# The first two pairs of a graph kernel in one written order on all engines

## The chip, the cores and the metric

The kernel runs on one core of one Trainium2 chip. The metric is the device time of one execution in microseconds; less is better. The engines of the core work side by side, each through its own list of instructions: TensorE (PE; its weight loads are shown apart as PEld), VectorE (DVE), ScalarE (ACT), GpSimd (POOL) and SyncE (SP, which here only issues transfers). An instruction that needs the result of another engine waits on a semaphore at the head of its own list.

## The reference, cut to what matters

The input is x with 128 graphs of 64 nodes and 768 features, and an integer adjacency of 128 x 64 x 64. There are two layers. The change lies in the first:

```python
h = relu(layernorm(x))
ctx  = (A @ (h @ Wadj.T + badj)) / deg + (A.T @ (h @ Wrev.T + brev)) / rdeg + h @ Wself.T + bself
rel  = (sum over j of A * E[rels]) @ Wr.T  + br * deg      # relation ids are the adjacency values
rel += (the same for the transposed adjacency) @ Wrr.T + brr * rdeg
x = x + ctx + rel
```

The second layer (attention over the graph and a gate) follows in a second phase that the change leaves alone.

## The kernel before

Rows are taken in tiles of 128 (two graphs), and tiles in pairs; there are 32 pairs. In the first phase each pair needs:

- `prep` and `prep_c`: the adjacency as float and bf16, and what the counting of relation ids needs;
- `norm` and `relu`: statistics of the tile on VectorE, a power on GpSimd, the relu on ScalarE;
- `degrees`: one small product on TensorE that sums the adjacency; then a reciprocal, and `over_degrees` writes the divided adjacency into `r`;
- `operands(p, k, q)`: TensorE multiplies h by r (so that the aggregation comes before the weights), ScalarE copies the result from PSUM; six such sets for a pair give the blocks a00 to a12 of the left operand A;
- `count`, `digits`, `count_t`: how often each relation id occurs in each row, on VectorE, then transposed by TensorE, so that the relation term becomes a product of counts with a small table;
- the products of A (2 x 3 blocks) with the weights B (3 x 3 blocks, three weight matrices side by side). From the second pair on this takes 15 block products instead of 18, with sums of blocks: `form` makes sums of A's blocks, `sum_of_weights` sums of B's blocks, once, in place. The first pair uses 18 plain products, since the sums aren't there yet.

```python
# (A block, B block, PSUM bank, first?, C block to add when done, sign, with counts?)
PRODUCTS = (("f1", "g6", "a", True, "11", "+", False), ("f7", "g10", "b", True, "00", "-", False), ...)
PLAIN = tuple((f"a{k}{j}", f"b{j}{q}", "abcdab"[2 * q + k], j == 0, f"{k}{q}" if j == 2 else None,
               "+", False) for q in range(3) for j in range(3) for k in range(2))
```

PSUM is divided: four banks a to d for the products, and two buffers `pb` that operands, degrees, count transposes and the table share. `add` takes a finished bank into x on VectorE:

```python
nc.tensor.matmul(bank[b][:, :CQ], OPS[p, an][:, q, s, :], bw[bn][...], ...)   # line 613
...
nc.vector.tensor_add(v, bank[b][:, :CQ], v)                                  # line 605 (607: minus)
```

`merged(main, side)` writes the six steps of each product down in order, and slips each side item in before the step whose number it names. A scheduler may then reorder the instructions of an engine; within `manual_schedule(engines=...)` those engines keep the written order. Before, only VectorE's first few instructions were held so:

```python
load(0)                       # adjacency and both x tiles of pair 0
nc.scalar.dma_start(et, e_t); # and five bias rows, on ScalarE's queue
for n in ("b00", "b10", "b20", "b01"): load_block(n)
load(1)
for n in ("b11", "b21", "b02", "b12", "b22"): load_block(n)
nc.sync.dma_start(wrt[0], wr_t); nc.sync.dma_start(wrt[1], wrr_t)
...
with tc.manual_schedule(engines={mybir.EngineType.DVE}):
    prep(0); deviation(X[0], ...); rd = degrees(0); scaled_mean(...)
    over_degrees(0, rd); deviation(X[1], ...); scaled_mean(...)
for k in range(2): relu(k, to[k])
operands(0, 0, 0); operands(0, 1, 0); prep_c(0)
late = ([(8 + 6 * i, operands(0, k, q)) for the other four sets]
        + [(20, build_table), (22, count(0, 0)), (24, count(0, 1)), (26, digits(0)),
           (60, count_t(0, 0)), (60, count_t(0, 1))]
        + [(i, sum_of_weights(bw, n)) for i, n in ((21, "g10"), (38, "u"), (45, "g12"), ...)])
for p in range(NP):
    more = [(3, finish(p - 1, ...))] if p else late
    merged(main(p), own(p) + side(p + 1) + more)
```

(Lambdas are written here as plain calls.) `build_table` scales the embedding rows (es), multiplies them by two weight tables and adds the biases: six float products into a `pb` buffer, a copy by ScalarE, then three bf16 parts split off by VectorE (a cast and a subtraction for each) and sent by SyncE into `tab`.

Of the kernel before, what the change touches and what calls it, by code (L numbers as in the profile page):

```python
# [72 lines left out]
PLAIN = tuple((f"a{k}{j}", f"b{j}{q}", "abcdab"[2 * q + k], j == 0, f"{k}{q}" if j == 2 else None,  # L73
               "+", False) for q in range(3) for j in range(3) for k in range(2))
# [58 lines left out]
def kernel(  # L133
# [104 lines left out]

    ident = const.tile([P, P], F32, name="ident")
# [115 lines left out]
    with ExitStack() as px:  # L355
# [7 lines left out]
        def load(p):  # L363
            if p >= NP:
                return
            AI[p] = work.tile([P, 2, 2, N], I32, name="ai")
            for d, src in ((0, adj), (1, adj_t)):
                nc.sync.dma_start(
                    AI[p][:, :, d, :],
                    src[p * 2 * GT : (p + 1) * 2 * GT].rearrange("(t g) i j -> (g i) t j", g=GT))  # L370
            for t in (2 * p, 2 * p + 1):
                X[t] = keep.tile([P, D], F32, name="x", bufs=6)
                nc.sync.dma_start(X[t], xf[t * P : (t + 1) * P, :])

        wrt = [keep.tile([P, D], F32, name="wrt", tag="x", bufs=6) for i in range(2)]
        load(0)
        et = wa.tile([P, NREL], F32, name="et")
        nc.scalar.dma_start(et, e_t)

        bia = keep.tile([5, D], F32, name="bia", tag="hf", bufs=2)  # L380
        for i, v in enumerate((br, brr, badj, brev, bself)):
            nc.scalar.dma_start(bia[i : i + 1, :], row(v, 1))

# [8 lines left out]
        for n in ("b00", "b10", "b20", "b01"):  # L392
            load_block(n)
        load(1)
        for n in ("b11", "b21", "b02", "b12", "b22"):
            load_block(n)
        nc.sync.dma_start(wrt[0], wr_t)
        nc.sync.dma_start(wrt[1], wrr_t)
        identb = wa.tile([P, P], BF16, name="identb")
        nc.vector.tensor_copy(identb, ident)  # L400
# [3 lines left out]
        for g in range(GT):  # L404
            s = slice(g * N, (g + 1) * N)
            nc.vector.memset(blkb[s, s], 1.0)

        vals = wa.tile([P, NG, N], BF16, name="vals")
        nc.gpsimd.iota(vals, pattern=[[1, NG], [0, N]], base=1, channel_multiplier=0,
                       allow_small_or_imprecise_dtypes=True)  # L410
        rts = []
        for i in range(2):
            r = wa.tile([P, 2, 3, N], F32, name=f"r{i}")
            for k in range(2):
                nc.vector.tensor_copy(r[:, k, 2, :], idc)
            rts.append(r)

# [3 lines left out]
        def build_table():  # L421
            ids = wa.tile([P, NV], F32, name="ids")
            nc.gpsimd.iota(ids, pattern=[[1, NV]], base=1, channel_multiplier=0,
                           allow_small_or_imprecise_dtypes=True)
            es = wa.tile([P, 2, NROW], F32, name="es")
            nc.gpsimd.memset(es, 0.0)
            for d in range(2):
                nc.vector.tensor_mul(es[:, d, d * NV : (d + 1) * NV],
                                     et[:, d * NB + 1 : (d + 1) * NB], ids)


            eb = wa.tile([5, NROW], F32, name="eb")
            nc.gpsimd.memset(eb, 0.0)
            nc.gpsimd.iota(eb[0:1, 0:NV], pattern=[[1, NV]], base=1, channel_multiplier=0,
                           allow_small_or_imprecise_dtypes=True)
            ebr = wa.tile([1, NROW], F32, name="ebr")
            nc.gpsimd.memset(ebr, 0.0)
            nc.gpsimd.iota(ebr[0:1, NV:NCNT], pattern=[[1, NV]], base=1, channel_multiplier=0,
                           allow_small_or_imprecise_dtypes=True)
            nc.sync.dma_start(eb[1:2, :], ebr)  # L440
            nc.sync.dma_start(eb[2:5, NCNT:NROW], ident[0:3, 0:3])
            pt = pss.tile([P, 2, 512], F32, name="pb")
            for hf in range(2):
                s = slice(hf * HALF, (hf + 1) * HALF)
                for d in range(2):
                    nc.tensor.matmul(pt[:NROW, hf, :HALF], es[:, d, :], wrt[d][:, s],
                                     start=(d == 0), stop=False)
                nc.tensor.matmul(pt[:NROW, hf, :HALF], eb, bia[:, s], start=False, stop=True)
            v = keep.tile([P, D], F32, name="tv", tag="hf", bufs=2)
            qs = work.tile([P, 2, D], BF16, name="tq", tag="eq", bufs=1)  # L450
            ql = keep.tile([P, D], BF16, name="tl", tag="hf", bufs=2)
            nc.scalar.copy(v[:NROW].rearrange("p (a b) -> p a b", a=2), pt[:NROW, :, :HALF])
            for i in range(3):
                q = qs[:, i] if i < 2 else ql
                nc.vector.tensor_copy(q[:NROW], v[:NROW])
                if i < 2:
                    nc.vector.tensor_sub(v[:NROW], v[:NROW], q[:NROW])
                for (a, b), tab in zip(PARTS, tabs):
                    nc.sync.dma_start(tab[i : 3 * (b - a) : 3, :], q[a:b, :])
# [8 lines left out]
        def norm(t):  # L468
            to = small.tile([P, 2], F32, name="rn")
            stats(X[t], to, behind=(t // 2 == 2))  # L470
            relu(t, to)

        def prep(p):

            af = ADF[p] = work.tile([P, 2, 2, N], F32, name="af", bufs=1)
            ins = nc.vector.tensor_copy(af, AI[p])
            if p == 2:
                tc.keep_in_program_order(ins)
            ab = AB[p] = work.tile([P, 2, 2, N], BF16, name="ab", bufs=1)
            nc.vector.tensor_copy(ab, af)  # L480
# [31 lines left out]

        def over_degrees(p, rd):

            nc.vector.reciprocal(rd, rd)
            for d in range(2):
                nc.vector.tensor_mul(rts[p % 2][:, :, 1 - d, :], ADF[p][:, :, d, :], rd[:, :, d, :])  # L517

        def count(p, k):

            eq = work.tile([P, 2, NG, N], BF16, name="eq", bufs=1)
            ins = nc.vector.tensor_tensor(
                eq, GR[p][:, k, :, None, :].to_broadcast([P, 2, NG, N]),
                vals[:, None, :, :].to_broadcast([P, 2, NG, N]), op=OP.is_equal)
            if p < 2 and k == 0:
                tc.keep_in_program_order(ins)
            nc.vector.tensor_tensor(
                eq, eq, WO[p][:, k, :, None, :].to_broadcast([P, 2, NG, N]), op=OP.mult)
            nc.vector.tensor_reduce(SUM[p][:, k], eq, AX.X, OP.add)
# [54 lines left out]
        def main(p):  # L584
# [44 lines left out]
            rest_of = ["12"] if p else ["12", "01", "11", "10", "00", "02"]  # L629
# [23 lines left out]

        def side(p):

            if p >= NP:
# [5 lines left out]
                    (9, lambda: over_degrees(p, degrees(p))),  # L662
# [15 lines left out]
        def own(p):  # L678

            if p == 0:  # L680
                return []
            return [(0, lambda: form(p, "f5", "f6", "f3")),
                    (10, lambda: form(p, "f10")),
                    (18, lambda: form(p, "f11"))]
# [3 lines left out]
        with tc.manual_schedule(engines={mybir.EngineType.DVE}):  # L688
            prep(0)
            to = [small.tile([P, 2], F32, name="rn") for k in range(2)]  # L690
            mv = [small.tile([P, 2], F32, name="mv") for k in range(2)]
            deviation(X[0], to[0], mv[0])
            rd = degrees(0)
            scaled_mean(to[0], mv[0])
            over_degrees(0, rd)
            deviation(X[1], to[1], mv[1])
            scaled_mean(to[1], mv[1])
        for k in range(2):
            relu(k, to[k])
        operands(0, 0, 0)  # L700
        operands(0, 1, 0)
        prep_c(0)
        late = ([(8 + 6 * i, lambda k=k, q=q: operands(0, k, q)) for i, (k, q) in enumerate(
                    ((0, 1), (1, 1), (0, 2), (1, 2)))]
                + [(20, build_table), (22, lambda: count(0, 0)),
                   (24, lambda: count(0, 1)), (26, lambda: digits(0)),
                   (60, lambda: count_t(0, 0)), (60, lambda: count_t(0, 1))]
                + [(i, lambda n=n: sum_of_weights(bw, n)) for i, n in (
                    (21, "g10"), (38, "u"), (45, "g12"), (50, "g6"), (54, "g14"), (60, "v"), (75, "w"),
                    (85, "g3"), (88, "g9"), (91, "g5"), (94, "g8"), (97, "g1"), (100, "g11"))])  # L710
        for p in range(NP):
            more = [(3, lambda: [f() for k in range(2) for f in finish(p - 1, k)])] if p else late
            if p == 1:
                more.append((10, row_constants))
            if p == NP - 1:
                more += fetch()
            merged(main(p), own(p) + side(p + 1) + more)


    with ExitStack() as px:  # L720
# [203 lines left out]
        def one_over(t):  # L924
            nc.vector.reciprocal(DN[t], DN[t])
# [161 lines left out]
        def parsed(order):  # L1087
            return [(n, int(k or 0)) for n, _, k in (x.partition("/") for x in order)]

        px.enter_context(tc.manual_schedule(engines={  # L1090
            mybir.EngineType.PE, mybir.EngineType.DVE, mybir.EngineType.Activation,
            mybir.EngineType.Pool}))
# [62 lines left out]
```

## Time and profile before

| | |
|---|---|
| time, median of 3 runs | 2501.05 us (2500.21 to 2501.13) |
| span of the profiled execution | 2500.9 us |
| TensorE busy | 2465.1 us, 99% |
| VectorE busy | 1972.9 us, 79% |
| ScalarE busy | 1073.7 us, 43% |
| first main product of pair 0 begins | 18.41 us |
| first main product of pair 2 begins | 137.33 us |
| VectorE busy from 0 to 137.33 us | 119.42 us |

A line of the order of time gives the start, the length, the engine, the line of the kernel, the operation, what it writes and reads, the shapes and how many instructions are put together; in brackets stands how long the engine was idle before it and which instruction released it. A float product of 256 columns is two records on TensorE. A line of a stretch gives its bounds and length, then busy us and instructions of PE, PEld, DVE, ACT and POOL, the mean granted clock of TensorE, the busy share of the transfer engines and GB/s.

### The profile page before, as it was taken

How to read it: one execution, taken by the hardware profiler on the slowest of the kernel's cores; microseconds unless marked ns; L12 is line 12 of the kernel's file. 1: busy time of each engine (PE TensorE's matmuls, PEld its weight loads, DVE VectorE, ACT ScalarE, POOL GpSimd, SP SyncE). 2: the span in 40 equal slices, each digit the busy share in tenths (PEclk: the TensorE clock that was granted, in tenths of full speed). 3: DMA queues.
4: the chain of work that ended last, by engine and by line, in shares of the span. 5: the costliest groups of instructions: out<-in, count | busy, mean ns of one | idle time of the engine just before them, and what ended most of it. 6: DMA issues, size and time to landing. Idle time of an engine off the chain costs nothing. (4 is left out here: it accounts for less than half of the span.)

```text
span 2500.9 us, 35441 instructions
## 1 busy us (share of the span) xinstructions
PE 2465.1 (99%) x12108; PEld 1730.6 (69%) x12108; DVE 1972.9 (79%) x4112; ACT 1073.7 (43%) x3588; POOL 439.5 (18%) x799
## 2 busy tenths in 40 slices
PE   7999999999999999999999999999999999999997
PEld 5888888888888888888888885444444444444445
DVE  7978677677777777776777655888888888888888
ACT  2122222222222222222222214777777777777777
POOL 0122121121121211211211201111111111111122
PEclk9999999999999999999999999999999999999998
DMA  5112122121131121221211243344444444444434
GB/s 181 55 65 94 53 84 75 53 103 56 53 106 53 59 100 53 78 81 53 93 66 51 102 132 128 97 110 109 109 104 110 104 104 104 113 108 104 106 88 95
DMA packets 116215, 224.58 MB, mean 90 GB/s; under 512 B 36554, under 2 KB 49981, under 8 KB 116034
## 3 DMA queue, kind: packets, MB, share of 16 engines
q1 hardware_dynamic: 106152, 197.48, 24.3%
q0 software_dynamic: 9728, 24.78, 6.4%
q8 instruction: 95, 1.56, 0.3%
q14 instruction: 86, 0.70, 0.1%
q10 hardware_dynamic: 154, 0.06, 0.0%
HBM read 96.07 MB, written 100.66 MB: 79 GB/s over the span
## 5 line engine op out<-in xcount | busy, mean ns | idle before, releaser
L613 PE MATMUL pwa<-weights,op 128*128 128x256 f32 x2304 | 542.1, 382 | 1.1 <-DVE x L605 1.1
L613 PEld LDWEIGHTS pwa<-weights,op 128*128 128x128 f32 x2304 | 423.3, 190 | 69.6 <-DVE x L605 9.0
L574 ACT COPY op<-pb 128x768 f32<-128x768 f32 x160 | 124.3, 798 | 753.9 <-PE pb L566 753.9
L613 PE MATMUL pwb<-weights,op 128*128 128x256 f32 x1536 | 369.4, 381 | 0.0
L308 DVE TENSOR_TENSOR op<-op 128x768 f32<-128x768 f32 x248 | 231.2, 952 | 153.5 <-ACT op L574 153.3
L613 PEld LDWEIGHTS pwb<-weights,op 128*128 128x128 f32 x1536 | 284.3, 190 | 45.8 <-issue 7.0
L806 PE MATMUL pma<-weights,op_f 128*128 128x512 f32 x620 | 307.6, 593 | 0.3 <-DVE weights L833 0.3
L858 ACT ACTIVATE pr<-pr 128x128 f32<-128x128 f32 x768 | 225.4, 296 | 25.0 <-DVE pr L848 24.9
L806 PE MATMUL pmb<-weights,op_f 128*128 128x512 f32 x372 | 191.2, 595 | 0.0
L806 PEld LDWEIGHTS pma<-weights,op_f 128*128 128x128 f32 x620 | 111.8, 190 | 112.9 <-issue 104.3
L282 POOL TENSOR_TENSOR rn<-ve,mhalf 128x1 f32<-128x1 f32 x128 | 107.6, 841 | 458.2 <-DVE ve L281 458.1
L613 PE MATMUL pwc<-weights,op 128*128 128x256 f32 x780 | 187.1, 383 | 0.0
L613 PE MATMUL pwd<-weights,op 128*128 128x256 f32 x768 | 178.5, 381 | 0.0
L566 PE MATMUL pb<-r,h 64*128 64x192 f32 x1536 | 155.4, 340 | 10.4 <-DVE r L517 7.2
L613 PEld LDWEIGHTS pwc<-weights,op 128*128 128x128 f32 x780 | 145.7, 190 | 25.3 <-issue 6.7
L545 POOL COPY c<-cnt 128x243 bf16<-128x243 bf16 x64 | 44.9, 731 | 663.0 <-PE pb L553 611.4
L613 PEld LDWEIGHTS pwd<-weights,op 128*128 128x128 f32 x768 | 146.2, 191 | 20.4 <-issue 0.7
L276 DVE BATCH_NORM_STATS2 st<-x 128x6 f32<-128x384 f32 x256 | 134.5, 547 | 30.7 <-DMA x<-in_x_dram 29.2
L566 PEld LDWEIGHTS pb<-r,h 64*128 64x128 f32 x1536 | 125.1, 189 | 47.0 <-issue 42.5
L643 ACT ACTIVATE hf<-x,rn 128x768 f32<-128x768 f32 x64 | 65.8, 1027 | 188.8 <-issue 128.3
L858 ACT ACTIVATION_READ_ACCUMULATOR pr<-pr 128x1 f32 x768 | 144.3, 188 | 0.0
L645 POOL TENSOR_TENSOR x<-x,hf 128x768 f32<-128x768 f32 x64 | 116.3, 1817 | 95.3 <-ACT hf L643 95.3
(207 smaller groups left out, 4280.3 us busy)
## 6 DMA issues: line engine op xcount, KB each, us to landing
x<-in_x_dram SPq DMA_DIRECT2D x64, 384.0 KB
h<-hf SPq DMA_DIRECT2D x64, 384.0 KB
out_dram<-x SPq DMA_DIRECT2D x64, 384.0 KB
hh<-hh SPq DMA_DIRECT2D x64, 384.0 KB
h<-h SPq DMA_DIRECT2D x64, 384.0 KB
x<-hh SPq DMA_DIRECT2D x64, 384.0 KB
out_dram<-f POOLq DMA_DIRECT2D x62, 384.0 KB, 5.2
hx<-weights SPq DMA_DIRECT2D x88, 192.0 KB
```

Of the source, the lines that this page charges most:

```text
L276: ins = nc.vector.bn_stats(st[:, i, :], src[:, i * HALF : (i + 1) * HALF])
L282: nc.gpsimd.tensor_tensor(to[:, 0:1], ve, mhalf, op=OP.pow)
L308: return (nc.vector.tensor_add if s1 == "+" else nc.vector.tensor_sub)(to, x, y)
L545: nc.gpsimd.tensor_copy(c3, CNT[p][:, k, :, None].to_broadcast([P, NROW, 3]))
L566: nc.tensor.matmul(ps[:, g, i * 3 * N : (i + 1) * 3 * N], H0[t][s, kb * P : (kb + 1) * P], rts[p % 2][s, k].rearrange("p s n -> p (s n)"), ...
L574: nc.scalar.copy(a.rearrange("p h s (g n) -> p g (h s) n", g=GT), ps[:, :, : 6 * N].rearrange("p g (x n) -> p g x n", n=N))
L613: nc.tensor.matmul(bank[b][:, :CQ], OPS[p, an][:, q, s, :], bw[bn][:, (s * KQ + q) * CQ : (s * KQ + q + 1) * CQ], start=(first and q == s ...
L643: nc.scalar.activation(h, X[t], AF.Relu, scale=to[:, 0:1], bias=to[:, 1:2])
L645: nc.gpsimd.tensor_add(X[t], X[t], h)
L806: nc.tensor.matmul(bank[p, b], OPS[p, an][:, q, :], bw2[bn][:, 2 * q * CQ : 2 * (q + 1) * CQ], start=(first and q == 0), stop=(q == KQ - 1 ...
L858: nc.scalar.activation(PR[t][:, j, h, :], PR[t][:, j, h, :], AF.Copy, accum_out=to)
```

## The change

Four things are done at once, all in the first two pairs:

1. The whole beginning, up to the end of the second pair's products, is written in one order for TensorE, VectorE, ScalarE, GpSimd and the issues of SyncE; from the third pair on the scheduler orders as before. Each side item has a place of its own in one of two lists (`first`, `second`).
2. The table products come before the first main product, between the first operand sets; the casts of the three parts go from VectorE to ScalarE. The loads they need (table weights, biases) go ahead of the weights, all on SyncE.
3. The 18 plain products run C block by C block (three in a row finish a block in one bank), columns in the order 0, 2, 1. Four of the six C blocks take their counts at once; two at the end of the pair, where all six did before.
4. The counting is cut in two (`ids_worth`, `ids_sum`), and reciprocal and scaled mean are placed apart.

It is meant to begin the main products with less in front of them, and to leave no hole between them while counts, sums and operands are made.

```diff
-               "+", False) for q in range(3) for j in range(3) for k in range(2))
+PLAIN = tuple((f"a{k}{j}", f"b{j}{q}", "abcdab"[2 * i + k], j == 0, f"{k}{q}" if j == 2 else None,
+               "+", i > 0) for i, q in enumerate((0, 2, 1)) for k in range(2) for j in range(3))
...
+    in_order = {PE, DVE, Activation, Pool}
+    written.enter_context(tc.manual_schedule(engines=in_order | {mybir.EngineType.SP}))
...
+        nc.scalar.dma_start(et, e_t)
+        load_adj(0)
+        load_x(0)
         nc.sync.dma_start(wrt[0], wr_t)
         nc.sync.dma_start(wrt[1], wrr_t)
+        for i, v in enumerate((br, brr, badj, brev, bself)):
+            nc.sync.dma_start(bia[i : i + 1, :], row(v, 1))
...
+        nc.sync.dma_start(eb[2:5, NCNT:NROW], ident[0:3, 0:3])
+        nc.sync.dma_start(eb[1:2, :], ebr)
+        load_block("b00")
+        load_x(1)
+        for n in ("b10", "b20", "b02", "b12"):
+            load_block(n)
+        load(1)
+        for n in ("b22", "b01", "b11", "b21"):
+            load_block(n)
...
-                nc.vector.tensor_copy(q[:NROW], v[:NROW])
+            nc.scalar.copy(q[:NROW], v[:NROW])
...
-            rest_of = ["12"] if p else ["12", "01", "11", "10", "00", "02"]
+            rest_of = ["12"] if p else ["00", "10"]
...
+        prep(0); scaled_rows(); rd = degrees(0); to, mv = deviations((0,)); one_over(rd)
+        mean_and_relu(0, to[0], mv[0]); over_degrees(0, rd)
+        table_product(0); operands(0, 0, 0); table_product(1); table_product(2); table_copy()
+        operands(0, 0, 1); prep_c(0); to, mv = deviations((1,))
...
+        first = [(0, ids_worth(0, 0)), (1, mean_and_relu(1, ...)), (2, ids_sum(0, 0)),
+            (4, operands(0, 0, 2)), (8, count(0, 1)), (12, operands(0, 1, 0)), (12, operands(0, 1, 1)),
+            (17, operands(0, 1, 2)), (18, table_part(0)), (19, weights_sums("g10")),
+            (20, table_part(1)), (22, digits(0)), (23, prep(1)), (24, devs(1)), (26, table_part(2)),
+            (28, degrees_and_norms(1)), (30, weights_sums("w", "v")), (36, weights_sums("g6")),
+            (38, weights_sums("u", "g14")), (38, count_t(0, 0)), (40, prep_c(1)), (44, count(1, 0)),
+            (45, count_t(0, 1)), (52, count(1, 1)), (54, operands(1, 1, 2)), ...]
+        second = [(0, form(1, "f5", "f6", "f3")), (7, prep(2)), (7, weights_sums("g9")),
+            (10, form(1, "f10")), (13, devs(2)), (18, form(1, "f11")), (20, degrees_and_norms(2)),
+            (25, weights_sums("g1")), (30, prep_c(2)), (32, ends[0]), (37, ids_worth(2, 0)), ...]
         for p in range(NP):
+            if p < 2:
+                more = (first, second)[p]
...
+            if p == 1:
+                written.close()
```

(Several lines are joined and lambdas written as plain calls; the rest of both lists goes on in the same manner, with the forms, operands and count transposes of the next pair. Two marks that hold pair 2's preparation in program order move to pair 3, and one for the counting of the first pairs is dropped.)

## The prediction

> **What bounds the kernel now.** I read the page first (busy shares, then the 40 slices), then the waits of TensorE alone, then the order of time on TensorE over the first 140 us, then busy time by stretch around the one hole there.
>
> The page says that TensorE is the bound nearly everywhere:
>
> ```profile
> PE 2465.1 (99%) x12108; PEld 1730.6 (69%) x12108; DVE 1972.9 (79%) x4112; ACT 1073.7 (43%) x3588; POOL 439.5 (18%) x799
> PE   7999999999999999999999999999999999999997
> DVE  7978677677777777776777655888888888888888
> ```
>
> Only the first slice (62 us) and the last show a PE digit below 9; the change touches the first two. VectorE is at 79% over the span but 9 tenths in slice 2: there it is nearly as tight as TensorE. The waits of TensorE over the whole run, longest first:
>
> ```profile
> PE pb L566 <- DVE r L517: 7.2, 1, 7.2
> PE pb L508 <- DVE ab L480: 4.4, 1, 4.4
> PE pb L553 <- POOL c L545: 3.2, 1, 3.2
> PE pb L566 <- ACT h L466: 3.2, 1, 3.2
> ...
> PE pwa L613 <- DVE x L605: 1.1, 1, 1.1
> ```
>
> (engine, tile and line, what it waited for: total us, times, longest.) These five add up to 19.1 us, and all lie before 138 us. Now the order of time on TensorE:
>
> ```profile
> 11.97 1.65 PE L566 MATMUL pb<-r,h 64*128 64x192 f32 x8 [7.18 <-DVE r L517]
> 16.83 1.65 PE L566 MATMUL pb<-r,h 64*128 64x192 f32 x8 [3.21 <-ACT h L466]
> 18.41 4.16 PE L613 MATMUL pwa<-weights,op 128*128 128x256 f32 x12
> ...
> 60.35 1.03 PE L613 MATMUL pwd<-weights,op 128*128 128x256 f32 x4
> 64.61 0.27 PE L553 MATMUL pb<-identb,c 128*126 128x128 bf16 x1 [3.24 <-POOL c L545]
> ...
> 70.42 2.03 PE L613 MATMUL pwd<-weights,op 128*128 128x256 f32 x4
> 72.28 2.76 PE L613 MATMUL pwa<-weights,op 128*128 128x256 f32 x12
> ...
> 137.33 2.86 PE L613 MATMUL pwa<-weights,op 128*128 128x256 f32 x12 [1.07 <-DVE x L605]
> ```
>
> The first main product starts at 18.41. Twelve matmul records take 4.16 us there and 2.76 us at 72.28, so the array is still slow at the start (by 1.5 us in that row). After the hole of 3.24 us, four records take 2.03 us instead of 1.03: slow again until about 72. The stretches confirm it (PE clock is the last figure but two):
>
> ```profile
> 62.00:64.00 2.00, 0.00 (x0) 0.00 (x0) 2.00 (x6) 0.00 (x0) 0.00 (x0) 1.00 0.00 0
> 66.00:68.00 2.00, 2.00 (x6) 1.11 (x7) 2.00 (x7) 0.27 (x1) 0.00 (x0) 0.50 0.00 0
> 70.00:72.00 2.00, 2.00 (x6) 1.31 (x5) 0.00 (x0) 0.84 (x2) 0.19 (x1) 0.50 0.00 0
> ```
>
> At 137.33 the third pair's products begin. From there on until the end of the first phase TensorE has no wait; pairs follow each other at 183.28 and 229.24, 45.95 us apart. So the question is one number: at what time does the third pair begin in the changed kernel? Whatever comes after is 2500.9 - 137.3 = 2363.6 us of the same work.
>
> **What the Trainium skill says.** "TensorE: Matmul & The Clock Gate", part 1 on the HAM clock gate: the array runs at half clock until about 3.4 us of sustained activity, and falls back after an idle window of about that length. The trace agrees: a hole of 3.24 us is followed by a granted clock of 0.50 from about 65 to 72. The same page, "Architectural detail", says that VectorE and ScalarE are strict first in, first out. The trace agrees: VectorE sat 3.19 us at 69.3 in front of one add that waited for TensorE, with nothing else slipped in. This is what makes a written order dangerous: a wait at the head holds everything behind it. "DMA: Bandwidth & Descriptors", "Issuing engines are not separate DMA queues": all issuing queues share the same engines, so moving the five bias loads from ScalarE's queue to SyncE's brings no bandwidth; in this trace each costs 0.23 to 0.53 us of issue.
>
> **The change part by part.**
>
> Start. Loads move about 350 GB/s from about 3 us on (345 to 354 in the stretches from 5 to 30). The adjacency lands at 3.75; both first x tiles have landed by 5.91. Now x of tile 0 comes alone behind the adjacency, 0.38 MB less, so about 1 us earlier: 4.9. VectorE: two casts 0.6 (to 4.4), two row scalings 0.3, the degree maximum 0.41 (to 5.3), two statistics 1.0, aggregate and add 0.35 (to 6.8), reciprocal 1.75 (to 8.5, the power of 0.57 on GpSimd hidden behind it), scaled mean 0.15, two products into r 0.5 (to 9.2). ScalarE's relu of 1.03 ends at about 9.8. Before, the first operand product waited until 11.97, because the reciprocal stood behind count preparation and copies. So it now starts 2 us earlier, at about 10.
>
> Table products. They are 12 records: 33.44 to 38.8 before, between other matmuls, some 0.36 us each, 4.3 us. Now 4 of them run before the first operand product (es and the first 0.38 MB table weight are there by about 6.5, when TensorE would idle), and 8 after it. Slow clock doubles part: 1.65 for the operand product (to 11.7), 4 records at about 0.5 (to 13.7), 4 at 0.36 (to 15.2), then the table's copy 0.8 on ScalarE, because the next operand product needs that PSUM buffer (two in all), then that product, 0.75: the first main product starts at 17 to 18, I take 17.5. That is only 0.9 earlier than before, but the table is done and the clock is up: 4.3 + 1.5 us less to come.
>
> First pair from 17.5. Start to start, 12 records take 2.59 us (77.89 to 80.48). 18 products: 46.6. Six table count groups at 0.22: 1.3. Ten operand sets: two together lengthen a product's stretch by 1.7 (108.30 to 112.59 is 4.29 against 2.59), singles by 0.95: 8.7. Four count transposes at 0.3: 1.2; the degrees 0.2. Sum 58.0, so 75.5 without a wait. The weights are no limit: in the new order of loads the last block, b21, lands after about 9.5 MB, at some 3 + 9.5/0.35 = 30 us, plus a few for the small issues; the block of the third C column to be formed is needed after 50.
>
> Count transposes. The hole of 3.24 at 61.4 came because the scheduled VectorE reached the digits of pair 0 only at 61.6 to 64. In the written order ids (1.02 + 1.02 + 1.88 per tile, twice 3.9) start at about 13 and end at 21, the digits (0.8) follow before step 23, the transposes stand at step 38. The hole goes, and with it the slow clock after it: 3.24 + half of 7 (65 to 72) = 6.8 us.
>
> New waits, from VectorE. Its list runs dry at 21.0, because the add of the first C block stands next in the order and that block ends only at 17.5 + 18 x 0.432 + four operand sets 3.4 = 28.7. Then come 0.42 (add), 0.95, 1.75 (g10), 0.95, 0.8 (digits), 0.6 (adjacency casts of pair 1): 5.5 us, 34.2. TensorE wants the degrees of pair 1 at step 28, at 28.7 + 10 x 0.432 = 33.0. Wait 1.2 us. Afterwards VectorE is behind: I count 43 us of its work from there to the end of the first pair (weight sums 12 x 1.75 = 21, ids 7.8, six forms 5.7, adds 2.1, preparation, statistics and reciprocal 8), so it ends at about 77, and TensorE at 75.5 + 1.2 = 76.7. They arrive together, and C block by C block each bank has whole blocks (7.8 us) of slack, so TensorE doesn't wait there.
>
> Second pair. TensorE needs 45.95. VectorE's written list: forms 4.75 and 4.75 (ten at 0.95), weight sums 3.5, preparation 2.9, statistics 2.75 and 2.8, degrees and norms 3.0, ids 7.8, digits 0.8, adds 16 x 0.42 = 6.7, small ones 0.5: about 41 us, 90%. Bank a is written by every third product or so, and the add in between must be done; following the list, the add of the fourth product falls at 91.6 on my scale when the seventh product wants its bank at 91.8 (both 0.8 later with the start at 76.7), and the adds of the seventh and the thirteenth come 0 to 0.6 late. I put 2 us on such waits, with the pair boundary.
>
> Sum: third pair at 17.5 + 58.0 + 1.2 + 45.95 + 2 = 124.6, against 137.3: 12.7 us earlier. Check by terms: table 4.3, start 0.9, slow start 1.5, hole and its slow clock 6.8, old boundary wait 1.1, two groups of count products and switching about 1.3, together 15.9, minus 3.2 of new waits: 12.7.
>
> The casts of the table go to ScalarE (3 x 0.56), which has idle time; that relieves VectorE by 1.7. What isn't free: the scheduled VectorE had run ahead into pair 3 by 137 (it cast the adjacency of pair 3 at 108.4). The changed one has no such lead when the written order ends. In later pairs VectorE has 34.2 of 45.6 us (stretch 137 to 183), so the lead comes back, but 0.5 to 1 us may go in the third pair. That leaves about 12 us: 2501 - 12 = 2489.
>
> **The rivals.** (a) *VectorE takes TensorE's place as bound in the first two pairs.* For it: 9.5 of 10 busy from 80 to 120 before, the dry 7.7 us at 21 in the new order, 90% in the second pair. Against it: the work of pair 3 (about 12 us) that was among that busy time is no longer due there, and the casts are gone. If each bank wait costs 1 us and a wait of over 3 us brings half clock again, 6 to 8 us go: 2495 to 2498. (b) *The start gets later*: all of SyncE's queue is one order, the bias loads and two small copies (0.74 and 0.95 us of issue) stand ahead of b00, and eight table records stand ahead of the second operand product at slow clock. If they all ran slow and the biases came late, the main products would start at 21: 2492. (c) *Nothing is lost to VectorE*: third pair at 121.5, 2485. (d) *The scheduler's order after the second pair differs and leaves a hole in each of the 30 pairs*: 0.3 us each would eat 9 us; the trace has not one such wait after 137, so I give it little.
>
> **Range and chances.** The middle is 2489. (c) sets the low end at 2484, (a) with a bit of (d) the high end at 2498. Two per cent are 50 us, while all idle and slow time of the first 137 us is about 27 us: faster by 2% is practically excluded, and so is slower, unless the order after the written part broke in every pair. 0.01, 0.98, 0.01.
>
> **What would show it.** The first main product at 17 to 18; table products ahead of it; no transposes waiting for GpSimd and no granted clock of 0.50 after the start; the degree product of pair 1 waiting about 1 us for ab; waits of pwa for x in the second pair, 2 us in all; pairs 45.95 apart after that, the third starting near 125. Wrong would be: a first main product after 20, a hole over 3 us, or waits of TensorE in every later pair.

## The result and the profile after

| | before | changed |
|---|---|---|
| time, median of 4 runs | 2501.09 us (2500.21 to 2501.23) | 2493.39 us (2492.51 to 2495.04) |
| ratio, 95% interval | | 0.9971 [0.9953, 0.9988] |
| first main product of pair 0 begins | 18.41 us | 14.49 us |
| third pair begins | 137.33 us | 125.78 us |
| span of the profiled execution | 2500.9 us | 2493.3 us |

The change saves 7.7 us, 0.3%. The page of the changed kernel, the rows of busy time and of the slices:

```profile
PE 2462.6 (99%) x12108; PEld 1727.9 (69%) x12108; DVE 1972.4 (79%) x4105; ACT 1075.8 (43%) x3591; POOL 441.5 (18%) x799
PE   8999999999999999999999999999999999999997
DVE  8887777777776776777777655888888888888888
```

The first slice of PE rises from 7 to 8; a slice is 62 us, so this row is too coarse for the rest. VectorE reads 8 in the first three slices, where it had 7, 9 and 7. The waits of TensorE in the changed kernel (engine, tile and line, releaser: total us, times, longest); the lines left out belong to the second phase, but for one of 0.3 (`pwb`):

```profile
PE pb L533 <- DVE ab L505: 6.2, 2, 4.2
...
PE pb L466 <- DMA wrt<-in_wr_t_dram: 2.3, 1, 2.3
PE pb L587 <- ACT cntT L589: 2.0, 5, 0.6
...
PE pwa L647 <- DVE x L639: 1.5, 1, 1.5
PE pwc L647 <- DVE op L315: 1.3, 1, 1.3
...
PE pwa L647 <- DVE x L641: 0.4, 1, 0.4
```

Of the 6.2 us in the first line, 4.2 are the wait at the very beginning, which was there before. The waits for `r`, `h` and `c`, 13.6 us together before, are gone. In their place stand many small ones. The order of time on TensorE says where:

```profile
6.92 2.82 PE L466 MATMUL pb<-wrt,es 128*81 128x384 f32 x4 [2.32 <-DMA wrt<-in_wr_t_dram]
9.68 1.14 PE L600 MATMUL pb<-r,h 64*128 64x192 f32 x8
...
14.49 1.99 PE L647 MATMUL pwa<-weights,op 128*128 128x256 f32 x8
...
32.64 0.28 PE L533 MATMUL pb<-ab,blkb 128*128 128x256 bf16 x1 [2.00 <-DVE ab L505]
...
37.87 0.22 PE L587 MATMUL pb<-identb,c 128*117 128x128 bf16 x1 [0.58 <-ACT cntT L589]
...
121.67 0.70 PE L647 MATMUL pwc<-weights,op 128*128 128x256 f32 x2 [1.29 <-DVE op L315]
...
124.92 1.03 PE L647 MATMUL pwb<-weights,op 128*128 128x256 f32 x4
125.78 2.75 PE L647 MATMUL pwa<-weights,op 128*128 128x256 f32 x12
...
140.99 2.86 PE L647 MATMUL pwa<-weights,op 128*128 128x256 f32 x12 [0.41 <-DVE x L641]
...
173.93 4.54 PE L647 MATMUL pwa<-weights,op 128*128 128x256 f32 x12 [1.46 <-DVE x L639]
```

Three things are to be seen. The table runs from 6.92, ahead of everything, and the main products begin 3.9 us earlier. Between 30 and 126 us lie seven holes, 5.3 us in all: the degrees (2.00), five transposes (0.58 and four times 0.35) and 1.29 at the end of the written part. And the third pair, which had no wait before, now ends in one of 1.46, after which twelve records take 4.54 us instead of 2.75.

The 1.29 is a wait for sums of A's blocks (line 315). In front of them VectorE had met this:

```profile
114.18 0.56 DVE L283 BATCH_NORM_STATS2 st<-x 128x6 f32<-128x384 f32 x1 [1.90 <-DMA x<-in_x_dram]
```

It is a statistic of the fourth pair, which the scheduler had slipped in among the written instructions, and its x hadn't landed. A bias row followed with 0.53 of wait. That these two made the hole is argued, not tested; run 7 below has neither them nor the hole.

The stretches behind the wait of 1.46 (PE clock is the last figure but two) show the slow clock:

```profile
174.00:175.00 1.00, 1.00 (x3) 0.82 (x4) 1.00 (x3) 0.97 (x2) 0.27 (x1) 0.50 0.06 16
...
177.00:178.00 1.00, 1.00 (x5) 0.84 (x4) 0.16 (x1) 0.23 (x1) 0.04 (x1) 0.79 0.60 233
```

The granted clock is 0.50 from 174 to 177 and comes back within the next microsecond. VectorE's own order of time shows what held it up:

```profile
145.38 0.18 DVE L568 CAST si<-sum 128x52 int32<-128x52 f32 x1
...
163.12 0.18 DVE L568 CAST si<-sum 128x52 int32<-128x52 f32 x1
...
172.58 0.14 DVE L288 TENSOR_SCALAR ve<-mv 128x1 f32<-128x1 f32 x1
173.38 0.16 DVE L293 SCALAR_TENSOR_TENSOR rn<-mv,rn 128x1 f32<-128x1 f32 x1 [0.66 <-POOL rn L289]
173.46 0.42 DVE L639 TENSOR_TENSOR x<-pwa,x 128x256 f32<-128x256 f32 x1
```

Line 639 is the add that frees bank a. It stands behind the closing statistics of the third pair's own first tile, which wait 0.66 us for GpSimd; the norm for the output follows on ScalarE:

```profile
173.62 1.03 ACT L677 ACTIVATE hf<-x,rn 128x768 f32<-128x768 f32 x1 [6.70 <-issue]
```

Line 568 ends the counting of one pair: two pairs are counted within this one.

To compare sequences with different starts I use two spans below: *opening*, from the first main product to the third pair, and *rest*, from the third pair to the same table product of a late pair, near 1400 us. Before, the rest is 1265.7; in the changed kernel 1269.55 (1395.33 - 125.78). One correction: where the end of the written part shows its wait of about 1.3 us, six records of the third pair (0.216 each; two of `pwc`, four of `pwb`) already run ahead of it, and before only two. So at equal work the third pair of the changed kernel begins at 124.9, and its rest lost 4.7, not 3.85.

### The profile page after: what moved, and what is told of

The parts are those of the page before. It is cut to its first block, busy times and chain, and to the rows that moved or that the text cites. A ratio compares the mean times of both kernels' runs of the same rounds, so it can differ in the third digit from the quotient of the medians.

```text
span 2493.3 us, 35434 instructions
## 1 busy us (share of the span) xinstructions
PE 2462.6 (99%) x12108; PEld 1727.9 (69%) x12108; DVE 1972.4 (79%) x4105; ACT 1075.8 (43%) x3591; POOL 441.5 (18%) x799
```

## The experiments

**The theories.** The gain reached at the third pair is near the one predicted; what is missing was lost after it. Theory A, the seam: where the written order ends, VectorE has no lead. The scheduler likes to be a pair ahead, and to get there VectorE has to count two pairs within one: the fourth and the fifth, ending at 145.38 and 163.12, while TensorE is at the third. So the adds that free banks come late. Before, this happened in the second pair, where line 534 ends two countings ahead of the wait of 1.07 for an add at 137.33:

```profile
108.94 0.18 DVE L534 CAST si<-sum 128x52 int32<-128x52 f32 x1
...
124.12 0.19 DVE L534 CAST si<-sum 128x52 int32<-128x52 f32 x1
```

Its rivals: the lost time lies in the small waits of the written part itself, or in VectorE having too much work altogether, or in a slow clock that no order cures. The recorded texts give the letters; A is the seam.

**1. Hold back the preparation of every later pair.** Two marks that keep an instruction in its place are set from pair 3 on, not for pair 3 alone. (The code counts pairs from 0: pair 3 is the fourth.)

```diff
-            stats(X[t], to, behind=(t // 2 == 3))
+            stats(X[t], to, behind=(t // 2 >= 3))
...
-            if p == 3:
+            if p >= 3:
                 tc.keep_in_program_order(ins)
```

> Only the two pins change: from pair 3 on, every pair's adjacency cast and first statistic stay behind what stands before them on VectorE, so no pair's counting is pulled a pair ahead. Theory A (in the changed kernel VectorE falls late in the third pair because the scheduler puts the counting of two pairs, about 12 us of extra VectorE work, into that one pair): the waits of 0.41, 0.28 and 1.46 us near 141 and 172 to 174 and the half clock after them vanish, pair 4 begins 4 us earlier relative to pair 3, total 2489.5. Rival B (VectorE is late simply because it is full from 80 us on and comes without a lead; whose work it is doesn't matter): waits of about 2 us remain near 172, total 2492 to 2493. Rival C (the lead is needed in every pair): holding makes TensorE wait in each of 30 pairs, total above 2500.

Measured: 2493.05 us (2490.64 to 2497.08, 5 runs), ratio 0.9966 [0.9954, 0.9979]. The order of time on TensorE of this kernel:

```profile
18.41 2.07 PE L647 MATMUL pwa<-weights,op 128*128 128x256 f32 x4
...
39.41 4.41 PE L647 MATMUL pwb<-weights,op 128*128 128x256 f32 x12
...
148.30 2.86 PE L647 MATMUL pwa<-weights,op 128*128 128x256 f32 x12 [0.41 <-DVE x L641]
...
178.81 2.86 PE L647 MATMUL pwa<-weights,op 128*128 128x256 f32 x12
```

The fourth pair, here at 178.81, begins without a wait and at full clock; the rest is 1265.9, 3.65 less than in the changed kernel at the same work, out of the 4.7 lost there. VectorE ends only one counting in the third pair's time (line 568 at 152.61). By its waits this is theory A; by the median, which hardly moved, it would be rival B. The 3.65 is read from one trace against another, and the times don't show it. The profiled execution, the slowest of the five, has losses elsewhere: it began its main products at 18.41, not 14.49, with the same instructions in front of them, and fell to half clock after the wait for the degrees (4.41 for twelve records). The written beginning has a spread of its own; runs 5 and 8 take it up.

**2. Hold back one pair more only.** The same marks for pairs 3 and 4.

```diff
-            stats(X[t], to, behind=(t // 2 == 3))
+            stats(X[t], to, behind=(t // 2 in (3, 4)))
```

> The pins hold for pairs 3 and 4 only, so the two pairs' counting that met in the third pair now meets in the fourth. Theory A: the third pair is free of waits, and the crowd moves to the fourth; as VectorE enters that one without being late, the wait there is shorter, 0 to 1.5 us, and total is 2489.5 to 2492. Rival B: no change against the changed kernel, 2493. Rival C: as theory A but with nothing gained by pinning all.

Measured: 2495.07 us (2492.86 to 2500.45, 9 runs), ratio 0.9976 [0.9966, 0.9985]. The third pair is free, and the crowd has moved on by exactly one pair:

```profile
226.38 4.54 PE L647 MATMUL pwa<-weights,op 128*128 128x256 f32 x12 [1.46 <-DVE x L639]
```

Two countings (line 568 at 198.21 and 215.25) lie in the fourth pair's time now. Same wait, same length, same slow clock, and the rest (1269.3) is as long as in the changed kernel. A shorter wait and at most 2492 were expected, and neither came. The lead that the scheduler takes has to be paid once, wherever the marks stop, unless they hold for every pair as in run 1.

**3. The degrees of pair 1 earlier.** The adjacency casts of pair 1 go from step 23 to step 17, ahead of the first add.

```diff
             (17, lambda: operands(0, 1, 2)),
+            (17, lambda: prep(1)),
...
-            (23, lambda: prep(1)),
```

> The adjacency cast of pair 1 goes ahead of the add of the first C block, into the stretch from 23.6 to 26.4 us where VectorE had nothing to do. If the wait of 2.0 us of the degree product at 30.6 to 32.6 is only that cast's place in the written order, it vanishes, the third pair begins at about 123.8, and total falls by 2 us to 2491.3. If the adjacency of pair 1 lands late (it was issued at 18.4 to 19.5 behind 5.5 MB), VectorE waits there instead and the add of the first block is late; then the degree product still waits about 1 us. If gains here are given back in the crowded third pair (VectorE not being any earlier), third pair 2 us earlier but total the same 2493.

Measured: 2493.74 us (2491.25 to 2498.7, 6 runs), ratio 0.9969 [0.9957, 0.9981]. The wait of 2.00 is gone, but that of the first transposes grew from 0.58 to 1.75. ScalarE's order of time shows what stood in front of the copy that the second half of the transposes waits for:

```profile
36.85 1.95 ACT L491 ACTIVATE h<-x,rn 128x768 f32<-128x768 f32 x2 [3.08 <-DVE rn L293]
38.70 0.24 ACT L589 COPY cntT<-pb 126x128 bf16<-126x128 bf16 x1
```

Two relus of pair 1, which had waited 3.08 us for VectorE, stand at the head. The opening is 110.0 against 111.3 in the changed kernel: 1.3 of the 2.0 us stay, the rest came back one item further down the list. The median shows nothing of it.

**4. The two halves of the transposes two steps apart.** `count_t` writes both halves into one `pb` buffer, one after the other, and each is copied by ScalarE. In the changed kernel the second half waits for the copy of the first.

```diff
-            (38, lambda: count_t(0, 0))
+            (38, lambda: count_half(0, 0, 0)),
+            (40, lambda: count_half(0, 0, 1))
```

(and so for the other five)

> The two transposes of a count, which share a PSUM buffer and wait for ScalarE's copy of the first half between them, stand two steps (4 matmul records, 0.9 us) apart. The five waits of 0.35 to 0.58 us (2.0 in all) vanish: the third pair begins at about 124, total 2491.5 if it isn't given back in the crowded third pair, 2493 if it is.

Measured: 2493.53 us (2490.06 to 2496.99, 5 runs), ratio 0.9965 [0.9953, 0.9978]. Products now lie between the halves:

```profile
44.26 0.22 PE L601 MATMUL pb<-identb,c 128*126 128x128 bf16 x1
44.31 1.08 PE L661 MATMUL pwc<-weights,op 128*128 128x256 f32 x4
45.23 0.22 PE L601 MATMUL pb<-identb,c 128*117 128x128 bf16 x1
```

All waits for `cntT` are gone. Against run 1, whose first main product came at the same time (18.41, here 18.32), the second pair begins at 81.81 instead of 83.90 and the third at 129.86 instead of 133.10. Two new waits for adds, 0.74 and 1.02, appear at 129.86 and 140.55: TensorE had caught up with VectorE. The median is that of the changed kernel again.

**5. A warm start.** 15 products of a tile of ones, whose result nobody reads, fill the gaps of TensorE before the first operand set (7 at the beginning, 4 after the degrees, 4 after the first table product).

```diff
+        def spin(n):
+            for _ in range(n):
+                nc.tensor.matmul(idle, ones[:, :P], ones, start=True, stop=True)
...
+        spin(7)
         prep(0)
```

> The changed kernel with 15 bf16 products of ones with ones (512 columns, result never read) added on TensorE where it is idle before the first operand set: 7 from about 1 us on, 4 behind the degrees, 4 behind the first table product. Theory W (the first 10 to 15 us of TensorE run at half clock, and when the clock rises differs from execution to execution[...]: main products began at 14.5, 16.6 and three times at 18.3 to 18.4 in five profiles with the same beginning): the main products begin at 13 to 14.5, the table products of the biases take 1.5 instead of 2.85 us, and the median falls by 2 to 4 us to 2490 to 2491, with a spread of about 2 us instead of 5 to 8. Rival (the spread comes from transfers that land at different times, not from the clock): start times keep spreading and the median stays at 2493.5.

Measured: 2492.51 us (2491.09 to 2492.68, 5 runs), ratio 0.9963 [0.9949, 0.9976]. The first main product comes at 14.26, and at 14.27 and 14.18 in runs 8 and 9, which have the same 15 products; without them five profiles of this beginning gave 14.49, 16.61, 18.32, 18.34 and 18.41. The median gains 1 us or so, within the intervals; the spread is 1.6 us, where runs 1 to 4 spread over 6.4 to 7.6 and the four runs of the changed kernel over 2.5. Late transfers aren't the reason for the late starts: in the four late profiles the table products began at 6.36 to 6.52, earlier than the 6.92 of the changed kernel, and it was the records from there on that took longer. So the late starts are a matter of TensorE's speed at the beginning.

**6. The table back among the main products.** The three table products and the copy go to step 14.

```diff
-        table_product(0)
         operands(0, 0, 0)
-        table_product(1)
-        table_product(2)
-        table_copy()
...
+            (14, lambda: ([table_product(i) for i in range(3)], table_copy())),
```

> The changed kernel with the six table products moved from before the first operand set to behind step 14 of the first pair, into the main products. If table products ahead are a gain of 4.3 us (TensorE had nothing else to do), total rises by 3 to 4 us to 2497. If they run at half clock there (8.5 us in three of five profiles) and only push the main products back, then without them the main products begin at 13, run 3.5 us at half clock and pay 4.3 us later: about equal, 2492.5 to 2494.

Measured: 2495.67 us (2494.97 to 2496.25, 10 runs), ratio 0.9977 [0.9968, 0.9987]. The order of time on TensorE:

```profile
12.57 3.34 PE L647 MATMUL pwa<-weights,op 128*128 128x256 f32 x8
...
22.82 2.74 PE L466 MATMUL pb<-wrt,es 128*81 128x384 f32 x8
25.49 1.51 PE L466 MATMUL pb<-bia,eb 5*81 5x384 f32 x4
```

Main products begin 1.9 us earlier, but slow (eight records in 3.34 instead of 1.99), and the table takes 4.1 us from 22.82 on. 4.1 + 1.35 - 1.9 = 3.5 us lost; the profile has the third pair at 128.97, 3.2 later, and the medians differ by 2.3, with intervals that overlap. So the table ahead is worth up to 3 us where the start is fast. Runs 1 and 2, with the table ahead but a late start, reach the third pair at 133.10 and 132.50, later than this run.

**7. No written order at all.** The changed program, with `manual_schedule` taken off: the scheduler orders everything.

```diff
-    written.enter_context(tc.manual_schedule(engines=in_order | {mybir.EngineType.SP}))
```

> The changed kernel without the written order: the program is written the same, but the scheduler orders all engines. If the written order is what brings the gain, the hole before the count transposes or one like it comes back (3 us and a stretch of half clock after it) and total is 2498 to 2503. If the gain comes from the new sequence of the program (table ahead, C block by C block) and not from forbidding the scheduler to move it, total stays at 2493.

Measured: 2489.64 us (2489.18 to 2490.99, 5 runs), ratio 0.9954 [0.9941, 0.9966]. All five runs lie below all runs of the changed kernel, and below all of run 5, measured beside it; neither expectation had it below 2493. The order of time on TensorE:

```profile
10.17 2.85 PE L465 MATMUL pb<-wrt,es 128*81 128x384 f32 x4 [5.77 <-DVE es L456]
...
17.83 1.99 PE L646 MATMUL pwa<-weights,op 128*128 128x256 f32 x8
...
123.72 2.86 PE L646 MATMUL pwa<-weights,op 128*128 128x256 f32 x12
...
171.58 2.86 PE L646 MATMUL pwa<-weights,op 128*128 128x256 f32 x12 [1.46 <-DVE x L638]
```

The scheduler begins later, since it has the scaling of the embedding rows late (5.77 of idle), and still reaches the third pair earlier. Its opening is 105.9 us. That of the written order is 111.3, or 110.4 at equal work: 4.5 more. The written order's holes (5.3) less the scheduler's single one (0.93, a relu at 26.12) make 4.4. The scheduler had no wait for the degrees, put other products between the halves of the transposes, and had no hole at the end of the second pair. It isn't its later start that spared it the wait for the degrees: in runs 1, 2 and 4 the main products began later still, at 18.3 to 18.4, and that wait was 1.99 to 2.00.

The wait at the end of the third pair is there too, and so are the two countings on VectorE within that pair:

```profile
143.38 0.18 DVE L567 CAST si<-sum 128x52 int32<-128x52 f32 x1
...
160.43 0.18 DVE L567 CAST si<-sum 128x52 int32<-128x52 f32 x1
```

So theory A has the crowd right and its place wrong: it needs no end of a written order. In all these kernels it stands where the marks stop. With the marks on pair 2 (before, run 10) two countings fall into the second pair, with the marks on pair 3 (the changed kernel, runs 3 to 7) into the third, with those on 3 and 4 (run 2) into the fourth, and with all pairs marked (runs 1, 8, 9, 11) into none. Nor does the slow clock belong to the written order: runs 4 and 6 have it, and after the same wait of 1.46, at 178.83 and 177.15, their twelve records take 2.86.

**8. All cures together.** Runs 1, 3, 4 and 5 in one kernel (15 products that nobody reads, as in run 5).

> Pins for all pairs, transposes apart, the adjacency cast of pair 1 early, and the warm start together. If the four losses are separate: third pair at about 120 (main products from 13.5, then 106.5), the rest 1265.8 to the end of the first phase, total 2484 to 2486. If VectorE takes over as the bound of the second pair (it was at 43 of 44 us there), the third pair begins at 122 to 123 and total is 2487 to 2488.

Measured: 2487.27 us (2485.7 to 2487.84, 5 runs), ratio 0.9942 [0.993, 0.9955]. This is the fastest version: 13.9 us below the kernel before, and all its runs lie below all others of this study except for an overlap of 0.08 us with run 11. What its waits of TensorE still have of the first pairs:

```profile
PE pwb L669 <- DVE x L663: 1.0, 1, 1.0
...
PE pb L609 <- ACT cntT L611: 0.8, 1, 0.8
...
PE pwa L669 <- DVE x L661: 0.6, 1, 0.6
```

The first main product comes at 14.27, the third pair at 121.13, an opening of 106.9, or 106.0 at equal work, as in run 7. The time is that of the second expectation: three waits are left, two of them for adds of VectorE and one for a copy that stands behind two relus, as in run 3.

**9. Written order for the beginning only.** It closes ahead of the first main product (`written.close()` before the loop over pairs), with the warm start and the marks of run 1: the early table of the written order with the scheduler's opening.

> The written order ends before the first main product instead of after the second pair; from there on the scheduler orders, with the pins for every pair from 3 on; the 15 warming products are kept. If the written order of the two pairs costs what the run with a free scheduler saved there (105.9 us from the first main product to the third pair against 111.3), and the fixed beginning with the warm array is worth keeping (main products from 14.3 instead of 17.8), the third pair begins at 119.5 to 120.5, the rest of the phase takes 1265.8, total 2483 to 2485. If the free scheduler's 105.9 came only from its later start (more of VectorE's work done by then), the third pair begins at 123 and total is 2487.5, as with all four together.

Measured: 2496.11 us (2493.46 to 2497.2, 11 runs), ratio 0.9977 [0.9968, 0.9986]. A miss: the start is as early (14.18), but there are two new holes, in the part that the scheduler orders. On TensorE:

```profile
27.11 1.01 PE L608 MATMUL pb<-r,h 64*128 64x192 f32 x8 [2.36 <-ACT op L616]
...
69.79 0.27 PE L595 MATMUL pb<-identb,c 128*117 128x128 bf16 x1 [4.30 <-ACT cntT L597]
```

and on ScalarE ahead of the copy that the second one waits for:

```profile
66.95 1.03 ACT L499 ACTIVATE h<-x,rn 128x768 f32<-128x768 f32 x1 [3.73 <-DVE ve L290]
...
69.49 0.25 ACT L597 COPY cntT<-pb 126x128 bf16<-126x128 bf16 x1
```

Relus of a later pair sat 3.73 us at the head of ScalarE's list and held a copy of 0.25 us. Both holes are followed by half clock (stretches from 28 to 30 and from 70 to 72: 0.50). Why the scheduler makes these holes here and not in run 7 isn't shown.

**10. C block by C block alone.** The kernel before, with the new order of the plain products and the loads and operands that go with it.

```diff
-               "+", False) for q in range(3) for j in range(3) for k in range(2))
+               "+", False) for i, q in enumerate((0, 2, 1)) for k in range(2) for j in range(3))
```

> The kernel before with one part of the change alone: the 18 plain products C block by C block in the columns 0, 2, 1, with loads, operand sets and one weight sum moved as that order needs; table, counts and the free scheduler as before. If the order of the blocks is what removes the hole before the count transposes, the third pair begins 6 to 10 us earlier and total is 2491 to 2495. If that hole comes from VectorE's order and the table's place, it stays, and total is 2499 to 2502.

Measured: 2500.86 us (2500.24 to 2502.19, 13 runs), ratio 0.9998 [0.999, 1.0006]. No gain: the transposes still wait, 2.23 us at 64.27 here, and the third pair begins at 136.81 instead of 137.33.

**11. No written order, later pairs held back.** Runs 7 and 1 together.

> The changed program with the scheduler free on all engines and the pins for every pair from 3 on. Against the free run (2489.6; it still waits 1.46 us near 171): the wait goes, total 2487.5. If the free scheduler puts the counting of pair 3 elsewhere anyway and the pins make new waits, 2489 to 2491.

Measured: 2489.22 us (2487.76 to 2489.51, 5 runs), ratio 0.9949 [0.9937, 0.9962]. No wait is left at the end of the third pair, and the rest is 1266.2 against 1267.6 in run 7. The medians differ by 0.4 and the ratios by 0.0005, some 1.3 us, both well within the intervals, so the times don't tell what that wait is worth.

## Why the prediction was right or wrong

The predicted time was 4.4 us too low, the range held. By its own steps, in the profiled execution of the changed kernel:

- *Start.* The first operand set at about 10: measured 9.68. Four table records ahead of it: so. The first main product at 17.5: measured 14.49. The 0.8 for the table's copy didn't come up: the second operand set follows the table without a gap (at 13.64, and at 16.83 in run 1). The array left its slow speed sooner: the first operand set took 1.14 instead of 1.65, the next table records 1.52 instead of 2.0. And the prediction's own steps end at 16.8, not at 17.5. In other executions of the same beginning it came at 16.6 to 18.4. The term was in the middle of its spread; the prediction hadn't said that it has one.
- *First pair, 58.0 and 1.2.* Measured 62.2 (14.49 to 76.68), 3.0 more. The degrees cost 2.00: from its add to the cast of the adjacency VectorE took 6.15 us instead of 5.5, as it waited 0.44 for ScalarE's cast of a table part and 0.25 for a transfer. That it ran dry at 23.6, not at 21.0, since the second x tile came late (3.08 us of wait for it at 14.17), cost nothing: it still stood idle for 2.86 in front of that add. Four waits of transposes, 1.6 us, were not foreseen at all: I had them at 0.3 each as pure work and overlooked that both halves share a buffer. The last 0.6 isn't traced.
- *The hole at the count transposes.* It is gone with its slow clock, as said. Runs 7 and 10 narrow down what it was: the block order alone doesn't remove it, the whole program without a written order does.
- *Second pair, 45.95 and 2.* Measured 48.2 at equal work (76.68 to 124.9). The size is right, the cause isn't: not one wait for an add, but 1.29 for sums of blocks at the end and 0.35 at a transpose.
- *Third pair, 0.5 to 1 us.* This is the term that was mis-sized most: it measured 4.7, made of waits of 0.41, 0.28 and 1.46, then 1.8 of half clock; the last 0.75 is in gaps too short for the view to mark. I had weighed VectorE's mean load, 34 of 46 us, but the scheduler rebuilds its lead within one pair. Runs 1 and 2 show it by removing it and by moving it. The mechanism in the prediction (VectorE has no lead when the written order ends) was right in part: VectorE does pay for a lead, but in the pair where the marks stop, and it does so without a written order as well (run 7). The 1.8 isn't a fixed price: runs 4 and 6 had the same wait without it.

The sum of the differences: start -3.0, first pair +3.0, second pair +0.3, third pair +3.95 (4.7 less 0.75), together +4.3; 2489.0 + 4.3 = 2493.3, the span of this profile. (The prediction started from a span of 2500.9, and both profiled executions, 2502.63 and 2495.04, took some 1.6 us more than their medians.) The start and the first pair cancel each other here by chance.

Some sums of the prediction are slightly off: 4.16 less 2.76 is 1.4, not 1.5; VectorE's work as listed adds up to 44.6 for the first pair, not 43, and to 40.25 for the second, not 41; from 80 to 120 it was busy for 9.7 tenths, not 9.5. None of this moves the result: VectorE stood idle for 2.91 us just before the adds that end the first pair (at 76.43).

Of the rivals, (a) came true in part: the time lies 1.6 below its range, and VectorE became the bound of single moments, not of the second pair. (b) happened in some executions (18.41 in run 1), never 21. (c) didn't, though run 8, with four losses removed, has the third pair at its 121. (d) didn't: after the third pair TensorE has no such wait. What I hadn't listed as a rival at all is the main lesson: that the new program might be good and the written order not. Run 7 shows that the scheduler alone gets more from it, 11.5 us instead of 7.7; with its four losses removed the written order gets 13.9 (run 8).

Open: the free order with the written order's early table was tried only as run 9, where two new holes spoilt it; an early scaling of the embedding rows in the free order wasn't tried, nor was the cut of the counting in two by itself. What removed the old hole at the transposes is known only as far as runs 7 and 10 go.

## What to carry to other kernels

A written order moves a wait to the head of every list behind it, so each item needs slack against the engine it waits for, and two uses of one buffer need other work between them; where a scheduler that runs ahead is held back for some pairs only, it takes its lead in the pair where the marks stop, so hold every later pair. Before crediting such an order, run the same program with the scheduler left free: here the program gained more without the order (run 7), and the order as first written cost some 4 us. Once TensorE is at 99%, a hole's price is its length plus the half clock that may follow it, so remove the longest holes first.

## What the runs showed of the hardware

- *The start of the clock isn't fixed.* With the same instructions from 6.5 to 7 us on, table records were fast from about 10.7 in the changed kernel (four in 1.52), but still slow at 14.05 in run 1 (four in 2.85), and its main products at 18.41 too (four in 2.07). The Trainium skill, "TensorE: Matmul & The Clock Gate", part 1 on the HAM clock gate, gives about 3.4 us of sustained activity. Run 5, with its dense products of ones, agrees better: slow from 1.46 (seven in 3.17), table records at 6.45 are faster (four in 1.87), and at 10.51 at full speed. In run 1 over 11 us of nearly unbroken small products (81 columns, 5 rows or 64 rows) didn't suffice. Whether it is their small size isn't shown. The granted clock in the stretches reads 1.00 throughout the start, in slow executions too; only the durations show it. That it is the same half clock is inferred from them: four main records took 2.07 at 18.41 in run 1, and 2.03 in the kernel before at 70.42, where the stretch reads 0.50.
- *A hole of 2 us may or may not bring half clock.* The wait for the degrees was 2.00 us in the changed kernel and 1.99 in run 1; afterwards twelve records took 2.75 in the one and 4.41 in the other, with a granted clock of 0.50 from 40 to 42. The wait of 1.46 (1.45 in run 3) was followed by twelve records in 4.54 in the changed kernel and in runs 2, 3 and 5, and in 2.86 in runs 4, 6 and 7. A wait of 1.75 in run 3 left the clock at 1.00 (stretches from 38 to 42). The same part of the page has an idle window of about 3.4 us; here less was enough in some executions. The page also says that the activity window runs freely, which would fit that the same hole falls differently in different executions; no run here shows where the window lies.
